# Gate biases of a recurrence: from three GpSimd additions to a one-hot matmul that opens the PSUM sum, and a wider clearance in the planner

## The chip, the cores and the metric

The kernel runs on one core of a Trainium2 chip. A core has five engines that run their own instruction queues in order and wait for each other through semaphores: TensorE (PE, matmuls into PSUM), VectorE (DVE), ScalarE (ACT), GpSimd (POOL) and SyncE (SP, which issues the DMAs here). The metric is the device time in microseconds of one execution of the whole program.

## The reference

Input `x` is 8 images of 56 x 56 pixels with 256 channels, all in float32. The program has two layers. Layer 0 normalizes in groups, routes each of the 49 regions (8 x 8 pixels) of an image to its 4 best regions, and does attention in which each query keeps only its 32 best of 256 keys; a 3 x 3 depthwise convolution of the values is added, and an output projection. Layer 1 sees the pixels of an image as a sequence of 3136 tokens: attention in a window of seven neighbours, then a recurrence over the tokens, each with a layer norm in front and a residual.

```python
def _L1_ffn_ref(x, U_i, V_i, b_i, U_f, V_f, b_f, U_c, V_c, b_c, U_o, V_o, b_o):
    xt = jnp.swapaxes(x, 0, 1)
    xi = xt @ U_i + b_i
    ...
    xg = xt @ U_c + b_c
    xo = xt @ U_o + b_o
    ...
    def step(carry, xs):
        h, c = carry
        xi_t, xf_t, xg_t, xo_t = xs
        i_t = jax.nn.sigmoid(xi_t + h @ V_i)
        f_t = jax.nn.sigmoid(xf_t + h @ V_f)
        g_t = jnp.tanh(xg_t + h @ V_c)
        o_t = jax.nn.sigmoid(xo_t + h @ V_o)
        c_new = h * c + i_t * g_t
        h_new = o_t * jnp.tanh(c_new)
        return ((h_new, c_new), h_new)
```

The gate `f_t` is computed and never used, so three gates are left. What the change touches are the input terms `xt @ U + b` of these three gates: 768 columns for each token.

## The kernel before

**Stages.** The work is cut into 56 units: seven rows of regions for each of eight images. A unit runs seven regions of the routed attention (scores on PE, eight rounds of MAX8 and MATCH_REPLACE8 on VectorE to find the 32 best, exponentials on ScalarE, a subtraction `pe - left` on GpSimd, lines 1004 and 1005, transposes and products on PE). A stream of "rows" steps follows a unit: output projection and residual (`project`; the bias `bo` is added to `x1` on GpSimd, line 1093), windowed attention (`window_attention`; the bias `bv1` is added on GpSimd, line 1192), layer norm, and at its end `gates(i)` for each block of 112 tokens (lines 1230 to 1252). `gates` transposes the normalized block (tile `xlT`), multiplies it with the gates' weights `wu` into two PSUM banks (512 and 256 columns, two matmuls each, since the 256 channels are two halves of the partitions), copies both on ScalarE to the tile `gs`, adds the bias `bu` in three GpSimd operations of 256 columns, and stores the block to DRAM (`xgd<-gs`). There are 224 such blocks, and 8 short ones of three tokens at the ends of the images. The banks come from `bank()`: two buffers for all of `rows`, `norm` (the first units' normalization, routing and keys) and the recurrence's output transposes.

**The recurrence** (lines 1338 to 1446) has 3136 steps in strict order, for all eight images at once. A step is a chain: `r_sum` (24 matmuls of the state with `r_v` into PSUM, on top of the input terms that were loaded back as `r_gin` and placed there), a tanh on ScalarE (`r_th`), a transpose on VectorE, a scan on VectorE (`r_c`, line 1394), a tanh on ScalarE (`r_tc`), and on VectorE the product that is the new state (`r_hs`, line 1405; called "the product" below). GpSimd then multiplies the new state with half the cell for the next step's scan (`r_cell<-r_hs,r_half`, line 1412). It starts once the first row of all eight images has its gates; from there on the steps run between the instructions of the attention, and the last ones run alone.

**The order is written out.** The class `_Plan` records every operation with a cost from `_time` (line 104: `held` is how long the engine is taken, `late` when the result is there) and lays all of them out in time by list scheduling (`run`, line 378); the order that comes out is the order of each engine's queue. On the chip only that order and the semaphores hold, not the planned times. In `run`:

- operations of the chain go as soon as they can; any other operation may start on an engine only if it would end by the time the chain is expected to need that engine, plus `SLACK` (line 63, 60 for GpSimd). For GpSimd the time that counts is that of the next chain operation with two SBUF operands, which is VectorE's scan or product, less `CLEAR` (lines 414 to 429).
- an operation of VectorE or GpSimd with two operands in SBUF that the plan itself made ("pair", line 341) is not started while the other engine runs one (line 449). Constants such as `bu`, `bo` and `bv1` are not the plan's tiles, so the three kinds of bias addition are not "pair".
- a GpSimd "pair" operation held over `LONG` may only start in the first part of a step (line 451).
- where PE would stand idle for more than `FILL`, a dummy matmul into `spare` is put in (lines 483 to 493 and 660 to 663). It computes nothing that is used.

`_halve` (line 520) halves the columns of two of the gates in `wu` and `bu`, since a sigmoid is computed as a tanh of half its argument.

Of the kernel before, what the change touches and what calls it, by code (L numbers as in the profile page):

```python
# [10 lines left out]
F32 = mybir.dt.float32  # L11
U32 = mybir.dt.uint32
AF = mybir.ActivationFunctionType
ALU = mybir.AluOpType
# [5 lines left out]
P = 128  # L20
C = 256
# [11 lines left out]
QB = 112  # L33
# [9 lines left out]
GATES = 3  # L43
# [15 lines left out]
FAR = 10**12  # L59
FILL = 220  # L60
LONG = 400
CLEAR = 250
SLACK = {"PE": 60, "DVE": 120, "ACT": 60, "POOL": 60, "SP": 1000}


# [174 lines left out]
class _Plan:  # L240
# [137 lines left out]
    def run(self, tc, fill):  # L378
# [35 lines left out]
        def expected(engine):  # L414
# [3 lines left out]
            for k in range(at, min(at + 7, len(chain))):  # L418
# [8 lines left out]
                if op.engine == engine or engine == "POOL" and op.pair:  # L427
                    return t - (CLEAR if engine == "POOL" else 0)
            return FAR
# [90 lines left out]
def _halve(nc, t, views):  # L520


    for v in views:
        for g in (1, 2):
            w = v.rearrange("p (j g u) -> p j g u", g=GATES, u=UJ)[:, :, g, :]
            nc.vector.tensor_scalar(w, w, 0.5, None, ALU.mult)
# [3 lines left out]
def _layers(ctx: ExitStack, tc, a, out):  # L530
# [9 lines left out]
    nc = tc.nc  # L540
    nb = x.shape[0]

    const = ctx.enter_context(tc.tile_pool(name="const", bufs=1))
# [14 lines left out]
    def bank():  # L558
        return ps_mm.tile([P, 512], F32, name="mm")
# [32 lines left out]
    def load(name, shape, src):  # L592
        t = const.tile(shape, F32, name=name)
        nc.sync.dma_start(t, src)
        return t
# [11 lines left out]

    bo = load("bo", [QB, C], a["bo"].to_broadcast((QB, C)))
    bv1 = load("bv1", [KB, C], a["bv1"].to_broadcast((KB, C)))
    bu = load("bu", [QB, GATES * C], a["br"].to_broadcast((QB, GATES * C)))  # L610
    _halve(nc, wu, [wu[:, k, :] for k in range(2)])
    _halve(nc, bu, [bu])

# [3 lines left out]
    for dy in range(3):  # L617
        rows = slice(dy * HD, (dy + 1) * HD)
        for n in range(24):
            k, dx, g = n // 12, n // 4 % 3, n % 4  # L620
# [28 lines left out]
    for t in sums:  # L649
        nc.tensor.matmul(  # L650
            t, gins[0].rearrange("p t g -> p (t g)")[:, :P], wu[:, 0, : t.shape[1]],
            start=True, stop=True, skip_group_check=True,
# [13 lines left out]
    raw, nc = nc, _Plan(tc)  # L666
# [396 lines left out]
    def layer_norm(i, src, by, nq=QB):  # L1063

        rs, off = by
        xl = two.tile([QB, C], F32, name="xln")
        nc.scalar.activation(
            xl[:nq], src, AF.Identity, bias=off[:nq, i : i + 1], scale=rs[:nq, i : i + 1]
        )
        pt = bank()  # L1070
        for k in range(2):
            nc.tensor.transpose(
                pt[:, k * QB : k * QB + nq], xl[:nq, k * P : (k + 1) * P], ident[:nq, :nq]
            )
        return pt[:, : 2 * QB].rearrange("p (k t) -> p k t", t=QB)[:, :, :nq]
# [58 lines left out]
    def window_attention(b, unit, im, row):  # L1134
# [95 lines left out]
        def gates(i):  # L1230
            q = sizes[i]
            xl = two.tile([P, 2, QB], F32, name="xlT")[:, :, :q]
            nc.scalar.copy(
                xl, layer_norm(i, row["t2"][:q, i, :], row["rs2"], q)
            )
            gs = two.tile([QB, GATES * C], F32, name="gs")[:q]
            for f, g in ((0, 2 * C), (2 * C, 3 * C)):
                pg = bank()
                for k in range(2):
                    nc.tensor.matmul(  # L1240
                        pg[:q, : g - f], xl[:, k, :], wu[:, k, f:g],
                        start=(k == 0), stop=(k == 1),
                    )
                nc.scalar.copy(gs[:, f:g], pg[:q, : g - f])
            for f in range(0, GATES * C, C):
                nc.gpsimd.tensor_tensor(
                    gs[:, f : f + C], gs[:, f : f + C], bu[:q, f : f + C], ALU.add
                )
            nc.sync.dma_start(
                xg[t0 // QB + i][:, :, b].rearrange("j g t u -> t (j g) u"),  # L1250
                gs.rearrange("t (j u) -> t j u", u=UJ),
            )
# [5 lines left out]
            + [lambda i=i: block(i) for i in blocks]  # L1258
            + [begin_gates]
            + [lambda i=i: gates(i) for i in blocks],  # L1260
        )

# [16 lines left out]
    for n in range(-(-SHIFTED // QB)):  # L1279
        q = min(QB, SHIFTED - n * QB)  # L1280
# [223 lines left out]
def _body(tc, a, out):  # L1504
    _layers(tc, a, out)
# [64 lines left out]
```

## Time and profile before

| what | value |
|---|---|
| time, median of 3 runs | 9194.27 us (9193.11 to 9199.71) |
| profiled execution, its own time | 9180.4 us |
| its span, first to last instruction | 9178.5 us |
| busy share of the span: PE, PE weight loads, DVE, ACT, POOL | 96%, 66%, 82%, 65%, 35% |
| granted clock of TensorE | 0.993 |
| bias additions `gs<-gs,bu` on POOL, full blocks | 672, mean 729 ns, busy 482.1 us |
| the same for the 8 short blocks | 24, mean 720 ns, busy 17.2 us |
| gates' matmuls, 512 columns, full blocks | 896 instructions, mean 636 ns, busy 491.9 us |
| gates' matmuls, 256 columns, full blocks | 896 instructions, mean 389 ns, busy 268.7 us |
| filler on PE (`spare<-ident`, line 661) | 14904 instructions, mean 276 ns, busy 2072.2 us |
| scan on DVE (`r_c<-r_cell`) | 3136, mean 290 ns, busy 910.8 us |

The trace is of one execution. "Busy" is the union of a group's instructions in time, so two overlapping instructions count once. A float32 matmul of the program shows as two instructions in the trace, and matmuls are pipelined, so their durations overlap. Every operation that the plan recorded has line 308, because the helper there issues them all; they are told apart by the names of their tiles (`out<-in`). The reason that is given for idle time is inferred from semaphores.

### The profile page before, as it was taken

How to read it: one execution, taken by the hardware profiler on the slowest of the kernel's cores; microseconds unless marked ns; L12 is line 12 of the kernel's file. 1: busy time of each engine (PE TensorE's matmuls, PEld its weight loads, DVE VectorE, ACT ScalarE, POOL GpSimd, SP SyncE). 2: the span in 40 equal slices, each digit the busy share in tenths (PEclk: the TensorE clock that was granted, in tenths of full speed). 3: DMA queues.
4: the chain of work that ended last, by engine and by line, in shares of the span. 5: the costliest groups of instructions: out<-in, count | busy, mean ns of one | idle time of the engine just before them, and what ended most of it. 6: DMA issues, size and time to landing. Idle time of an engine off the chain costs nothing.

```text
span 9178.5 us, 500794 instructions
## 1 busy us (share of the span) xinstructions
PE 8792.1 (96%) x203918; PEld 6037.0 (66%) x203918; DVE 7559.4 (82%) x32392; ACT 5939.4 (65%) x23551; POOL 3221.5 (35%) x7747
## 2 busy tenths in 40 slices
PE   7999999999999999999999999999999999999999
PEld 4555556666666666666666666666666666688888
DVE  5776799999999899999899999899999999734443
ACT  4665667776666677676676676677766766534444
POOL 1232344444343343343344443434434444311111
PEclk9999999999999999999999999999999999999999
DMA  6545433333332333333333333233333232210000
GB/s 198 155 129 163 111 106 82 93 92 80 93 91 78 91 84 90 89 85 91 88 82 92 91 82 90 78 93 88 83 92 89 80 90 78 60 28 23 23 24 21
DMA packets 1071271, 798.40 MB, mean 87 GB/s; under 512 B 402366, under 2 KB 1001524, under 8 KB 1068964
## 3 DMA queue, kind: packets, MB, share of 16 engines
q1 hardware_dynamic: 1068964, 766.36, 30.8%
q8 instruction: 1604, 26.28, 1.2%
q14 instruction: 703, 5.76, 0.2%
HBM read 527.08 MB, written 238.88 MB: 83 GB/s over the span
## 4 chain that ended last, share of the span: by engine, by line
PE 52%; DVE 25%; ACT 6%; issue 2%; DMA 1%; SPq 0%; POOL 0%; ACTq 0%; DVEq 0%; POOLq 0%
PE r_sum L308 19%; PE mm L308 15%; PE spare L661 12%; DVE left L308 8%; DVE top L308 6%; DVE r_c L308 3%; PE pt_av L308 3%; PE sc L308 3%; DVE r_cell L308 2%; DVE r_hs L308 2%; ACT pe L308 1%; ACT r_th L308 1%; ACT xln L308 1%; DVE st L308 1%; ACT r_sum L308 1%
## 5 line engine op out<-in xcount | busy, mean ns | idle before, releaser
L308 PE MATMUL r_sum<-r_v,r_hs 128*16 128x64 f32 (+2 forms) x150528 | 2758.0, 220 | 160.4 <-DVE r_hs L308 107.1
L308 PEld LDWEIGHTS r_sum<-r_v,r_hs 128*8 128x8 f32 (+2 forms) x150528 | 2224.2, 96 | 907.8 <-DVE r_hs L308 802.6
L308 POOL TENSOR_TENSOR r_cell<-r_hs,r_half 128x16 f32<-128x16 f32 x3136 | 706.7, 225 | 4012.7 <-DVE r_hs L308 3192.8
L661 PE MATMUL spare<-ident 128*32 128x128 f32 x14904 | 2072.2, 276 | 6.2 <-issue 4.5
L308 DVE MATCH_REPLACE8 left<-top,left 128x256 f32<-128x256 f32 x4704 | 1903.3, 408 | 0.0
L308 DVE MAX8 top<-left 128x8 f32<-128x256 f32 x4704 | 1848.2, 413 | 1.8 <-POOL r_cell L308 0.3
L308 ACT ACTIVATE r_th<-r_sum 128x64 f32<-128x64 f32 x3587 | 802.3, 224 | 1559.4 <-PE r_sum L308 1507.1
L661 PEld LDWEIGHTS spare<-ident 128*32 128x32 f32 x14904 | 1474.8, 110 | 309.6 <-issue 263.4
L308 DVE STREAM_TRANSPOSE r_cell<-r_th 128x64 f32<-128x64 f32 x3136 | 812.8, 259 | 882.5 <-ACT r_th L308 842.2
L308 POOL TENSOR_TENSOR pe<-pe,left 128x256 f32<-128x256 f32 x1568 | 1136.2, 729 | 821.5 <-ACT left L308 397.9
L308 ACT ACTIVATE r_tc<-r_c 128x16 f32<-128x16 f32 x3136 | 696.9, 222 | 717.4 <-DVE r_c L308 696.0
L308 DVE TENSOR_TENSOR_SCAN r_c<-r_cell 128x48 f32<-128x48 f32 x3136 | 910.8, 290 | 86.9
L308 ACT ACTIVATE pe<-sc,nmax 128x256 f32<-128x256 f32 x1568 | 710.9, 470 | 185.5 <-DVE left L308 105.3
L308 ACT ACTIVATE left<-left,nmax 128x256 f32<-128x256 f32 x1568 | 773.8, 502 | 13.8 <-DVE left L308 7.8
L308 PE MATMUL pt_av<-ident,pe 128*128 128x128 f32 x3136 | 691.2, 289 | 49.4 <-ACT pts L308 19.4
L308 PE MATMUL mm<-wu,xlT 128*112 128x256 f32 (+3 forms) x1856 | 732.6, 512 | 2.6 <-ACT xlT L308 1.7
L308 DVE MAX8 top<-sc 128x8 f32<-128x256 f32 x1568 | 620.4, 416 | 80.8 <-PE sc L308 80.4
L308 ACT ACTIVATE r_half<-r_c 128x16 f32<-128x16 f32 x3136 | 655.3, 209 | 0.0
L308 DVE SCALAR_TENSOR_TENSOR r_hs<-r_cell,r_tc 128x16 f32<-128x16 f32 x2685 | 545.4, 203 | 124.5 <-ACT r_tc L308 103.4
L308 DVE MATCH_REPLACE8 left<-top,sc 128x256 f32<-128x256 f32 x1568 | 641.2, 412 | 0.7 <-issue 0.6
L308 ACT COPY pts<-pt_av 128x256 f32<-128x256 f32 x1568 | 574.8, 367 | 97.6 <-PE pt_av L308 89.5
L308 PEld LDWEIGHTS pt_av<-ident,pe 128*128 128x128 f32 x3136 | 375.3, 143 | 349.2 <-issue 190.0
(131 smaller groups left out, 12151.6 us busy)
## 6 DMA issues: line engine op xcount, KB each, us to landing
kg<-kd SPq DMA_DIRECT2D x1568, 64.0 KB
vg<-vd SPq DMA_DIRECT2D x1568, 64.0 KB
vshift<-lines SPq DMA_DIRECT2D x336, 232.0 KB
xgd<-gs SPq DMA_DIRECT2D x224, 336.0 KB
r_gin<-xgd SPq DMA_DIRECT2D x1568, 48.0 KB
xchunk<-xt SPq DMA_DIRECT2D x112, 448.0 KB
lines<-v SPq DMA_DIRECT2D x112, 290.0 KB
xn<-xh SPq DMA_DIRECT2D x56, 560.0 KB
```

What stands on the lines that cost most here:

```text
L308: made[:] = [method(*[v.real() if isinstance(v, _View) else v for v in args], **{k: v.real() if isinstance(v, _View) else v for k, v in kw ...
L661: raw.tensor.matmul(spare[:32, :P], ident[:, :32], ident, start=True, stop=True, skip_group_check=True)
```

## The change

The additions on GpSimd are removed. Instead a constant matrix `bu` of 128 partitions holds the bias in its first row and zeros in the others, and a constant column `pick` is one in its first row and zero in the others. A matmul of `pick`, spread over the block's tokens, with `bu` gives the bias for each token; it opens the accumulation of each of the two PSUM banks (`start=True`), and the two matmuls of the weights add to it. The load of `bu` becomes one row in place of a copy to 112 partitions. Separately, the planner's constant `CLEAR` goes from 250 to 450.

```diff
-CLEAR = 250
+CLEAR = 450
...
-    bu = load("bu", [QB, GATES * C], a["br"].to_broadcast((QB, GATES * C)))
+    bu = const.tile([P, GATES * C], F32, name="bu")
+    nc.vector.memset(bu, 0.0)
+    nc.sync.dma_start(bu[0:1, :], a["br"])
+    pick = const.tile([P, 1], F32, name="pick")
+    nc.vector.memset(pick, 0.0)
+    nc.vector.memset(pick[0:1, :], 1.0)
...
             for f, g in ((0, 2 * C), (2 * C, 3 * C)):
                 pg = bank()
+                nc.tensor.matmul(
+                    pg[:q, : g - f], pick.to_broadcast((P, q)), bu[:, f:g], start=True, stop=False
+                )
                 for k in range(2):
                     nc.tensor.matmul(
                         pg[:q, : g - f], xl[:, k, :], wu[:, k, f:g],
-                        start=(k == 0), stop=(k == 1),
+                        start=False, stop=(k == 1),
                     )
                 nc.scalar.copy(gs[:, f:g], pg[:q, : g - f])
-            for f in range(0, GATES * C, C):
-                nc.gpsimd.tensor_tensor(
-                    gs[:, f : f + C], gs[:, f : f + C], bu[:q, f : f + C], ALU.add
-                )
             nc.sync.dma_start(
                 xg[t0 // QB + i][:, :, b].rearrange("j g t u -> t (j g) u"),
                 gs.rearrange("t (j u) -> t j u", u=UJ),
```

## The prediction

> **What bounds the kernel now.** I read the busy slices first, then the busy time by stage, then the groups of the middle stage, then the timeline around single steps.
>
> The slices of the span (40 equal ones, tenths busy) show three stages: a head without recurrence, a long middle, and a tail in which VectorE is 40% busy.
>
> ```profile
> PE   7999999999999999999999999999999999999999
> DVE  5776799999999899999899999899999999734443
> POOL 1232344444343343343344443434434444311111
> ```
>
> By stage (start:end, length, then busy us and instructions of PE, PEld, DVE, ACT, POOL, then granted clock, DMA share and GB/s):
>
> ```profile
> 0.00:1340.00 1340.00, 1191.84 (x8321) 705.94 (x8322) 975.89 (x3858) 796.82 (x2278) 393.82 (x732) 0.96 0.52 144
> 1340.00:7970.00 6630.00, 6399.55 (x162175) 4289.48 (x162173) 6107.11 (x26291) 4606.32 (x18589) 2672.57 (x6395) 1.00 0.32 87
> 7970.00:8230.00 260.00, 258.52 (x6841) 216.26 (x6840) 95.44 (x409) 98.94 (x465) 45.10 (x146) 1.00 0.12 32
> 8230.00:9178.00 948.00, 942.22 (x26589) 825.36 (x26586) 381.00 (x1837) 437.29 (x2222) 109.99 (x474) 1.00 0.08 23
> ```
>
> The middle holds 72% of the span (6630 of 9178.5) and there VectorE works 6107 of 6630 us. The trace has 2571 steps between 1345 and 7960 us, so 2.573 us a step; the tail has 443 steps in 940 us, 2.122 each. So the middle is bound by VectorE together with the serial chain of a step. PE's 6400 us are no bound: 1102.9 of them are filler.
>
> ```profile
> L661 PE MATMUL spare<-ident 128*32 128x128 f32 x7456 | 1102.9, 277 | 4.7 <-issue 4.5
> L308 PE MATMUL mm<-wu,xlT 128*112 128x512 f32 (+2 forms) x1560 | 619.0, 511 | 0.2
> ```
>
> What GpSimd costs is not its own time but what it does to two VectorE operations of the chain. Groups of the middle (xcount | busy, mean ns | idle before):
>
> ```profile
> L308 POOL TENSOR_TENSOR pe<-pe,left 128x256 f32<-128x256 f32 x1314 | 952.7, 729 | 283.2 <-ACT left L308 250.9 <-ACT pe L308 1.0 <-issue 0.3
> L308 POOL TENSOR_TENSOR gs<-gs,bu 112x256 f32<-112x256 f32 x567 | 408.1, 729 | 57.0 <-ACT gs L308 43.1 <-issue 1.6
> L308 DVE TENSOR_TENSOR_SCAN r_c<-r_cell 128x48 f32<-128x48 f32 x2571 | 773.8, 301 | 75.4
> L308 DVE SCALAR_TENSOR_TENSOR r_hs<-r_cell,r_tc 128x16 f32<-128x16 f32 x2571 | 525.1, 204 | 94.5 <-ACT r_tc L308 74.2
> L308 DVE MAX8 top<-sc 128x8 f32<-128x256 f32 x1310 | 522.1, 416 | 1.9 <-PE sc L308 1.5
> ```
>
> The same stage's medians are 258 ns for the scan and 175 for the product (r_hs): (301-258)*2571 = 110 us and (204-175)*2571 = 75 us are stalls. The timeline shows two of them (start, length): the scan stretched from 0.26 to 0.73 us beside a bias addition, the product from 0.18 to 0.44 beside a `pe` subtraction; each ends as GpSimd ends.
>
> ```profile
> 4808.89 0.73 POOL L308 TENSOR_TENSOR gs<-gs,bu 112x256 f32<-112x256 f32 x1
> 4809.01 0.73 DVE L308 TENSOR_TENSOR_SCAN r_c<-r_cell 128x48 f32<-128x48 f32 x1
> 5004.25 0.73 POOL L308 TENSOR_TENSOR pe<-pe,left 128x256 f32<-128x256 f32 x1 [1.62 <-ACT left L308]
> 5004.57 0.44 DVE L308 SCALAR_TENSOR_TENSOR r_hs<-r_cell,r_tc 128x16 f32<-128x16 f32 x1
> ```
>
> I went through the trace and put every scan or product over its median by 40 ns to the GpSimd operation beside it. Scans: `pe` 193 for 65.1 us, `gs` 141 for 34.5, `x` 32 for 9.3, `v` 9 for 2.6, `sum` 17 for 2.1. Products: `pe` 213 for 63.4, `v` 26 for 11.3, `gs` 27 for 3.7, `sum` 18 for 2.0, `x` 5 for 0.8. Together 194.8 us, `gs` 38.2 of it. This is all that the change can win on VectorE. A stall holds VectorE and the chain at once, so a microsecond saved is one off the end if the middle keeps its steps, and 2.12/2.57 = 0.83 if it keeps its length; I count 1.
>
> **The change, part by part.** *The additions go* (224 blocks of three, and 8 short blocks): 38.2 us of stalls with them. The other end is 0: the 204 steps of the middle with just one `gs` beside them average 2.432 us, those with no long operation 2.524, so there is no sign that an addition by itself costs a step. I take **-38**, the direct count.
>
> *Less crowding.* 48 scans were hit by a `pe` (12.3 us) and 28 by an `x` (8.1) that had started back to back behind another GpSimd operation. Without the additions that queue is shorter. **-20**; ends 0 and -20.
>
> *CLEAR 250 to 450.* In the plan the scan stands 231+925+260+276 = 1692 ns behind the product's start. A 256-column operation is held 728, so it may start up to 1692-250+60-728 = 774 ns behind the product, and after the change up to 574. But on the chip nothing ties GpSimd to the product: it starts when its queue and its data allow. The `pe` row waits 250.9 us for ScalarE's `left`, and the operation at 5004.25 started before the product that the plan puts it behind. A rule of the plan that lateness overrides should do little. Ends: all the rest of the stalls goes, -(194.8-38.2-20.4) = -136; or the 352 long operations that started 0.6 to 0.8 us behind a product's end are pushed into the next one at 63.4/213 = 0.30 us each, +105. I take **0**, between them. The new limit binds `nmax` and the power of the scales too (held 184 and 1050; the latter may start until 252 ns behind the product, before 452). `nmax` feeds ScalarE's `pe`, which frees the scores' banks; VectorE idles 1.5 us in the whole middle for new scores (the MAX8 row), for seven more rounds of work lie in between. With that cover gone it would be 656*0.2 = 131 us. Cost 0.
>
> The Trainium skill (SBUF — State Buffer, "Who interferes with whom") says that a VectorE operation with two SBUF inputs and a GpSimd operation that reads SBUF exclude each other, and that the one that issues second blocks until the first ends. A random hit on 729 ns would then cost 0.36 us, 168 hits of `gs` 61 us and the sum below -55; the trace's own hits average 38.2/168 = 0.23, so I keep the count.
>
> *The new matmuls.* Each block gets one more of 512 and one of 256 columns beside two of each, so half of the `mm<-wu,xlT` row: 619.0/2 = 310 us of PE in the middle, under the 1102.9 of filler. The cover is not perfect, since a matmul before `r_sum` delays it. From the product's end to the first `r_sum` matmul the fastest twentieth of the steps takes 54 ns, the mean 121: (121-54)*2571 = 172 us, caused by 6399.6-1102.9-2278.1 (the `r_sum` row) = 3019 us of other PE work, 0.057 each. 310*0.057 = **+18**. Ends: 0, and 390 matmuls each delaying a step by 0.28 (the worst class, 49 steps behind a 56-column `mm<-xn,w`: 333 ns in place of 54), +109. The first matmul of a group needs no `xlT`, so it waits for a bank alone and may take one of the two early, holding it through the 0.34 us `xlT` copy; behind it on PE stand `r_sum` and the scores. Nobody else of the middle uses these banks but `r_hx`'s transposes, once in 16 steps, for an output nobody waits for. Weights are loaded beside matmuls. In the price above.
>
> *Head.* 31 blocks by 491.9/448+268.7/448 = 1.70 us is 53 us more PE, where PE had 177 us of filler and 148 idle, and VectorE 364 idle. Between 53*0.057 = 3 and 53; nearer the lower, since PE's real work is (1192-177)/1340 = 76%. **+8**.
>
> *Start and queues.* One 3 KB row behind a memset in place of a 112-row load on SP; first use at 351 us. `xgd<-gs` on SP waits for ScalarE's copy and no longer for three additions: earlier, and the recurrence reads it a row of images later. 0. After 8070 us no gates are left: 0.
>
> **Sum:** -38-20+0+18+8 = -32 us. The profiled execution took 9180.4 (span 9178.5), so 9148; the median of the runs is 9194.27, 13.9 above it, so **9162**.
>
> **Rivals.** (a) *All collisions go*: -195+26 = -169, 9025. For it: 46% of the long operations start over 0.8 us behind a product, which a tighter rule is aimed at. Against: their data set their start. (b) *PE takes the place of GpSimd*: the new matmuls stand in front of `r_sum` at the worst class's price, +109 in the middle and +53 in the head, less 58: +104, 9298. It decides from (58-8)/390 = 0.13 us for each new matmul on. For it: PE without filler is 80% busy in the middle. Against: mean delay per step is 67 ns with four times as much work. (c) *The freed slots fill*: `pe` moves to where `gs` stood and meets the scan as often, so no stall goes: 0+26, 9220. For it: long operations number 2602 in 2571 steps, so slots are sought after; against: their own number falls by a fifth. (d) *Gains and costs cancel*, within 18 us.
>
> **How the numbers follow.** My forecast's case (-18 to -100) 0.42; (a) 0.10; (d) 0.16; (b) and (c) together 0.32. Two tenths of a per cent, 18 us, is about what this kernel's measurement tells from nothing. Faster 0.52, same 0.16, slower 0.32. The range 9070 to 9250 leaves 0.07 below, for most of (a), and 0.13 above, for (b); the forecast alone spans 9094 to 9176.
>
> **What would show it.** The scan's mean in the middle falls from 301 toward 285 ns, the product's stays near 204 (its stalls are `pe`'s lateness). Filler falls by about 300 us. Mean product-to-`r_sum` stays within 10 ns of 121. First `r_sum` of the recurrence at 1338 us moves under 15. Wrong if the scan and the product both drop to their medians, or if the step grows while filler is still there, or if the head grows by more than 40.

## The result, and the profile after

The changed kernel takes 9249.2 us (median of 5, 9239.2 to 9254.0), the kernel before 9194.3 on the same chip: a ratio of 1.0054, interval 1.0043 to 1.0065. It is slower, by 55 us; a gain of 32 had been forecast. The profiled execution has a span of 9252.1 us against 9178.5, 73.6 more: the one before lies 14 us under its median, the one after 5 us over its own.

The busy slices of the changed kernel, 40 equal ones:

```profile
PE   7999999999999999999999999999999999999999
DVE  5777799998888899898999998899899988844443
POOL 1222233333333333333333333333333323311111
```

VectorE's full stretch now lasts longer, and its fall to 4 comes later: the last MAX8 or MATCH_REPLACE8 of the attention ends at 8174 us in place of 7942. By stage (start:end, length, then busy time and instructions of the engines, granted clock, DMA share and rate):

```profile
0.00:1340.00 1340.00, 1212.06 (x8752) 710.77 (x8756) 988.44 (x3917) 812.47 (x2331) 334.03 (x653) 0.95 0.52 145
1340.00:7970.00 6630.00, 6428.14 (x160619) 4266.26 (x160609) 5961.75 (x25723) 4499.34 (x18242) 2205.24 (x5706) 1.00 0.32 85
7970.00:8230.00 260.00, 252.56 (x6377) 168.32 (x6366) 196.66 (x845) 159.67 (x665) 74.54 (x200) 1.00 0.24 63
8230.00:9178.00 948.00, 937.84 (x25331) 811.57 (x25332) 371.62 (x1774) 432.61 (x2153) 109.89 (x456) 1.00 0.10 25
```

VectorE is busy for less of the middle window than before (6107 us there): it gets less of the attention done in it. The two groups that the prediction was about, in the same window (busy, mean ns, idle before):

```profile
L308 DVE TENSOR_TENSOR_SCAN r_c<-r_cell 128x48 f32<-128x48 f32 x2568 | 734.5, 286 | 75.0
L308 DVE SCALAR_TENSOR_TENSOR r_hs<-r_cell,r_tc 128x16 f32<-128x16 f32 x2568 | 533.1, 208 | 117.7 <-ACT r_tc L308 100.8
```

The scan's mean has come down from 301 ns as forecast: the stalls beside the additions are gone. Counted as in the prediction, over the first 2500 steps, all stalls of scan and product fall from 189 to 161 us; the 36 us beside additions are gone, and those beside other GpSimd operations have grown by 8. The new matmuls on PE, all of them (count, then shortest, median and longest in ns, first and last in us, the commonest shapes), and then the filler in the middle window:

```profile
L308 PE MATMUL mm<-bu,pick x928: 378/591/1062, 348.1 to 8294.2; 128*112 128x256 f32 x92, 128*112 128x512 f32 x86, 128*3 128x512 f32 x8
```

```profile
L666 PE MATMUL spare<-ident 128*32 128x128 f32 x6576 | 962.6, 278 | 8.6 <-issue 8.5
```

A new matmul takes 0.59 us at the median, and the filler still has 963 us of the middle: by PE's room alone there was place for them.

I split the time of both profiles along the chain, step by step (first product; then, for the first 2500 steps, each wait and each operation; then the rest):

| us, total | before | after | difference |
|---|---|---|---|
| first product at | 1340.6 | 1316.3 | -24.3 |
| steps over 8 us, beyond 2.57 each | 0 | 24.4 | +24.4 |
| product's end to the first `r_sum` matmul | 303.6 | 383.7 | +80.1 |
| `r_sum` until the tanh starts | 2476.1 | 2452.2 | -23.9 |
| wait for the transpose | 224.8 | 208.3 | -16.5 |
| scan | 753.1 | 716.3 | -36.8 |
| product | 510.9 | 518.8 | +7.9 |
| wait for the second tanh | 188.3 | 176.2 | -12.1 |
| from step 2500 to the last product | 1398.0 | 1470.4 | +72.4 |

So the loss is not in the ordinary steps. Three steps wait long: 20.1 us at step 444, 9.4 at 1788 and 54.0 at 2684 (at 8234 us). Without what these take beyond 2.57 us, the first 2500 steps last 6435 us before and 6436 after: the 80 us more before `r_sum` are made up by the rows below it. The three waits are 76 us; another 21 come from the other steps after 2500, beside which the attention now runs on; the earlier start gives 24 back.

Step 2684 is followed by the first that needs tokens of the last row of regions. In the kernel before, the last gate copies of the seven rows were done at steps 1, 430, 865, 1301, 1733, 2168 and 2619, while the recurrence needs the rows' first tokens from steps 0, 445, 893, 1341, 1789, 2237 and 2685 on: up to the sixth row, every row gave it some 13 steps more of a lead. (The last row has one short block more for each image; its first blocks, which come into use first, were all done at 2608.) In the changed kernel the copies are done at 4, 448, 899, 1346, 1792, 2238 and 2691, and the last row's first blocks at 2685. The recurrence has caught up with its own input. The queue of SyncE shows it (start, length): the stores `xgd<-gs` stop, then the first block of the eighth image is stored, and right behind it the input terms `r_gin` of the next steps are loaded.

```profile
8204.22 23.23 SPq L308 DMA_DIRECT2D xgd<-gs  x4
8275.57 0.32 SPq L308 DMA_DIRECT2D xgd<-gs  x1
8278.86 3.14 SPq L308 DMA_DIRECT2D r_gin<-xgd  x8
```

Then ScalarE places the terms in PSUM, and `r_sum` starts again:

```profile
8284.85 0.48 ACT L308 COPY r_sum<-r_gin 128x128 f32<-128x128 f32 x2
8285.81 0.69 PEld L308 LDWEIGHTS r_sum<-r_v,r_hs 128*8 128x8 f32 x48 [0.77 <-ACT r_sum L308]
```

At 444 and 1788, too, the loads of the next terms begin only after the wait has begun (2467.2 and 5939.9 us; the waits begin at 2456.9 and 5937.5). These are the waits that ended last around step 2684:

```profile
POOL r_cell L308 <- DVE r_hs L308: 33.2, 7, 20.6
DVE r_cell L308 <- ACT r_th L308: 25.5, 7, 19.1
POOL v L308 <- ACT v L308: 24.3, 5, 11.5
```

Columns: engine and what waits, what it waits for, then total, times and longest in us. The chain's own pair, the copy on GpSimd behind the product and the scan behind the tanh, stands there seven times in these 70 us, where steps of 2.57 us would give 27, and the longest of them last 20.6 and 19.1 us: the engines of the recurrence stand idle. The waits name only the last releaser; that the gates are late is read from the gate copies, stores and loads above.

### The profile page after: what moved, and what is told of

It is laid out like the page before. It is cut to its first block, busy times and chain, and to the rows that moved or that the text cites. A ratio compares the mean times of both kernels' runs of the same rounds, so it can differ in the third digit from the quotient of the medians.

```text
span 9252.1 us, 498048 instructions
## 1 busy us (share of the span) xinstructions
PE 8899.4 (96%) x202968; PEld 6017.4 (65%) x202968; DVE 7546.9 (82%) x32395; ACT 5935.8 (64%) x23551; POOL 2732.1 (30%) x7051
## 4 chain that ended last, share of the span: by engine, by line
PE 59%; DVE 18%; ACT 6%; issue 2%; DMA 1%; POOL 0%; SPq 0%; ACTq 0%; DVEq 0%; POOLq 0%
PE r_sum L308 21%; PE mm L308 20%; PE spare L666 11%; DVE left L308 6%; DVE top L308 4%; PE pt_av L308 4%; PE sc L308 3%; DVE r_c L308 2%; DVE r_hs L308 2%; DVE r_cell L308 2%; ACT r_th L308 1%; ACT xln L308 1%; ACT pe L308 1%; ACT left L308 1%; ACT r_tc L308 0%
## 5 line engine op out<-in xcount | busy, mean ns | idle before, releaser
L308 PE MATMUL r_sum<-r_v,r_hs 128*8 128x64 f32 (+2 forms) x150528 | 2749.5, 220 | 156.4 <-DVE r_hs L308 92.7
L666 PE MATMUL spare<-ident 128*32 128x128 f32 x13026 | 1797.9, 276 | 10.2 <-issue 8.5
L666 PEld LDWEIGHTS spare<-ident 128*32 128x32 f32 x13026 | 1298.1, 110 | 244.3 <-issue 208.2
L308 DVE TENSOR_TENSOR_SCAN r_c<-r_cell 128x48 f32<-128x48 f32 x3136 | 872.6, 278 | 86.3
L308 PE MATMUL mm<-wu,xlT 128*112 128x256 f32 (+2 forms) x1856 | 744.6, 513 | 0.0
```

The costliest lines, as they stand in the source:

```text
L308: made[:] = [method(*[v.real() if isinstance(v, _View) else v for v in args], **{k: v.real() if isinstance(v, _View) else v for k, v in kw ...
L666: raw.tensor.matmul(spare[:32, :P], ident[:, :32], ident, start=True, stop=True, skip_group_check=True)
```

## Why the rows are late: reading the serial path

The "rows" stream has two banks and works through projection, windowed attention, gates, and then the next unit's values and convolution, one after the other. Mean over units 12 to 46 of four kernels, in us:

| stretch | before | after | matmuls, CLEAR 250 | no bias, CLEAR 250 |
|---|---|---|---|---|
| last addition to `sum` until the unit's first projection matmul | 34.3 | 58.8 | 41.1 | 49.0 |
| first projection matmul to first gate copy | 71.3 | 71.7 | 69.6 | 70.1 |
| first gate copy to last | 25.3 | 30.7 | 32.9 | 24.7 |
| last gate copy to the convolution of the next but one unit | 37.3 | 36.3 | 34.3 | 36.6 |
| convolution to the next unit's projection | 5.9 | 5.2 | 5.5 | 5.5 |

The last four follow each other without a gap and add up to the unit's time, 140.0 us before (sum of the rounded rows: 139.8). The first row says that the attention is done 34 us before its projection begins, so the attention is not what the rows wait for; it is the other way round, for the first addition to `sum` follows the convolution's copy by 0.1 to 0.9 us on average in these kernels. The rows' work is a serial path, and PE's filler hides nothing on it. The recurrence takes 448 steps of 2.57 us for a row of eight units, 143.9 us a unit, so this path had 3.9 us to spare. The new matmuls add 5.4 to 7.6 us to the gates' phase; the other stretches give part of it back. The whole unit takes 142.3 us with the matmuls alone, 143.4 with CLEAR alone (not in the table), and 143.9 with both: each part by itself leaves a little of the 3.9 us, both leave nothing. That this is why the two lose only together is argued from these means; a mean alone does not tell the loss, for one kernel below (matmuls, CLEAR 260) has 143.9 too and is not slow.

CLEAR lengthens the same path at another place. From the last mean and variance to the normalization that uses them (two GpSimd operations and one of VectorE lie between) it takes 2.83 us before, 3.64 after; 3.51 with CLEAR 450 alone, 2.87 with the matmuls alone. The power itself has the same length, only later; first the changed kernel's row in the middle, then that of the kernel before:

```profile
L308 POOL TENSOR_TENSOR rs<-rs,mhalf 112x4 f32<-112x4 f32 x85 | 88.1, 1037 | 5.0
```

```profile
L308 POOL TENSOR_TENSOR rs<-rs,mhalf 112x4 f32<-112x4 f32 x87 | 90.2, 1037 | 7.1
```

Both have a mean of 1037 ns: it is the start that CLEAR moves, not the length.

## The experiments

Ratios are to the kernel before, run beside each kernel; in brackets the 95% interval. That kernel took 9202.5 us beside the first four kernels below (the two parts apart) and 9191 to 9195 beside the others, so kernels of different groups are compared by ratio. "The wait" is that at step 2684 in the profile, which is one execution and not always a typical one.

**The two parts apart.** CLEAR alone, the matmuls alone, and no bias at all at both values (these two leave the gates' bias out).

```diff
-CLEAR = 250
+CLEAR = 450
```

> The kernel before with CLEAR 450 alone; the additions stay on GpSimd. Theory A (the new matmuls on PE take the loss, CLEAR does nothing): same as before, 9194 within 15 us, rows of gates done at steps 430, 865, 1301 as before. Theory B (the narrower GpSimd window takes the loss): as slow as the changed kernel, 9249, the attention ends near step 2660 and the recurrence waits for a row's gates at steps 444 and 2684. Theory C (each part slows the attention, and time is only lost where the recurrence then runs out of tokens): between, near 9220, with a wait at step 2684 shorter than the changed kernel's 54 us.

Measured: 9205.6, ratio 1.0003 [0.9994, 1.0012]; rows complete at 439, 887 and so on, the wait 17.9 us. Theory A has the time, but the rows are late and a wait is there, as C had it; ordinary steps that are 21 us shorter make up for part of it.

> The changed kernel with CLEAR back at 250: only the bias matmul is new. Theory A: 9249, as the changed kernel. Theory B: faster than before by the stalls beside the additions, about 9160 to 9180. Theory C: near 9200; the attention is slower than before, the recurrence waits at step 2684 for less than 54 us.

Measured: 9161.4, ratio 0.9949 [0.9935, 0.9963]: faster than before. Waits of 25.5 at step 444 and 19.5 at 2684, in a profiled execution of 9188.4 us, the slowest of the five; the other four took 9154 to 9163.

> Leaves the gates' bias out altogether (neither addition nor matmul), CLEAR 250: what the additions cost, without the price of their replacement. All theories: faster than before; by my count of stalls beside the additions 38 us and by less crowding 20 more, so 9136 to 9160. If the additions cost nothing of the end time: 9194.

Measured: 9180.5, ratio 0.9971 [0.9958, 0.9983]; no wait. This is above the 9136 to 9160 of the forecast: a gain of some 27 us where 58 had been counted.

> Leaves the gates' bias out altogether, CLEAR 450. Theory A: as with CLEAR 250. Theory B: slower than with CLEAR 250 by about 55 us. Theory C: without additions GpSimd has room, so slower than with CLEAR 250 by under 15 us, and no wait at step 2684.

Measured: 9164.7, ratio 0.9955 [0.9941, 0.9968]; no wait.

Where the time goes in these profiles, in us ("waits" is what steps over 8 us take beyond 2.57):

| | before | after | CLEAR alone | matmuls alone | no bias, 250 | no bias, 450 |
|---|---|---|---|---|---|---|
| first product at | 1340.6 | 1316.3 | 1353.6 | 1330.8 | 1335.1 | 1339.5 |
| first 2500 steps without waits | 6434.8 | 6435.8 | 6413.6 | 6393.7 | 6437.0 | 6429.1 |
| waits | 0 | 75.8 | 15.4 | 39.9 | 0 | 0 |
| steps from 2500 on without waits | 1398.0 | 1419.0 | 1419.1 | 1417.1 | 1380.3 | 1385.4 |

What follows: neither part is slow alone. The matmuls alone win 0.5%, CLEAR alone does nothing, CLEAR without any addition or matmul does no harm either, and the two together lose 0.54%. With the matmuls in, CLEAR costs 1% (0.9949 to 1.0054); at CLEAR 450 the matmuls cost 1% against no bias at all (0.9955 to 1.0054), and at 250 they cost nothing (0.9971 to 0.9949). Theories A and B fall. C had the direction, but its 9200 for the matmuls alone was 40 too high. Of the 66 us between the profiles of the changed kernel and of the matmuls alone, 36 are waits and 42 ordinary steps, less 15 at the start; why the steps are shorter at CLEAR 250 is open.

**More and less on PE.** The bias matmul cut to 8 columns and overwritten by the weights' product (this leaves the bias out), and issued twice.

```diff
-pg[:q, : g - f], pick.to_broadcast((P, q)), bu[:, f:g], start=True, stop=False
+pg[:q, :8], pick.to_broadcast((P, q)), bu[:, f : f + 8], start=True, stop=True
...
-                        start=False, stop=(k == 1),
+                        start=(k == 0), stop=(k == 1),
```

> The changed kernel, CLEAR 450, with the bias matmul cut to 8 columns and overwritten by the weights' matmul: the gates' bias is left out; the number, order and waits of the matmuls stay. Theory R (the matmuls' length lies on the serial path of the rows' work, which at 140.0 us a unit before was 3.9 us under the 143.9 that the recurrence leaves it): the gates' phase of a unit falls from 30.7 back to about 25 us, no wait at step 2684, 9160 to 9190. Theory S (a matmul that holds a bank early or blocks PE is what costs): as the changed kernel, 9249, with the wait.

Measured: 9232.7, ratio 1.0046 [1.0032, 1.0060]. As theory R wants, the gates' phase is 25.3 us, the rows are early (431, 862, ... 2579) and there is no wait; but the time is 43 us above R's range. The loss is in the steps: product to `r_sum` 393.0 us in the first 2500 steps, against 343.5 with no bias at all.

```profile
L308 PE MATMUL mm<-bu,pick x928: 169/243/354, 342.7 to 8016.3; 128*112 128x8 f32 x178, 128*3 128x8 f32 x8
```

The row gives a likely cause: the planner prices such a matmul at 5*8/3+50 = 63 ns, while its two instructions hold the next matmul back for about 130 ns (medians: 31 ns between their starts, 98 more to the next start; their lengths of 0.24 us overlap), so the planner squeezes it in front of `r_sum`. In 120 of the first 2500 steps the last matmul ahead of `r_sum` is one of the bias or one of the gates' weights behind it, and the gap is 36 us in all; with no bias it was 15 steps and 1 us. That is 35 of the 50 us more. Twice more, with other values of CLEAR:

> The short bias matmul (8 columns, overwritten; the gates' bias left out) with CLEAR 250. If the many short matmuls themselves cost (the bank taken early, PE's order): 9220 to 9245, as with 450. If 9233 was CLEAR's or the order's doing: as without any bias, 9155 to 9190. No wait at 2684 in either case.

Measured: 9275.0, ratio 1.0084 [1.0066, 1.0103]; rows early, no wait. This is above both forecasts, and the same count gives only 13 us here, so the gap before `r_sum` does not explain the slowest of the three.

> The same with CLEAR 440. If 9233 was a poor order and no mechanism: 9160 to 9210; if the short matmuls cost: 9220 to 9245. No wait at 2684.

Measured: 9229.3, ratio 1.0038 [1.0024, 1.0052]. So it was no poor draw of one order: the kernels with these short matmuls lose 0.4 to 0.8%, 35 to 77 us, to the kernel before without the rows being late. That their price in the plan is the cause is argued, for two of the three, and not shown; a kernel with the true price was not run.

> The matmul version with CLEAR 250 (9161), each bias matmul issued twice. Theory R: 6.4 us more in each of 48 units, nothing of it in slack, so some 300 us more, 9430 to 9520, with waits of about 50 us where each row of gates is late (steps near 444, 892, 1340, 1788, 2236, 2684). Theory of the prediction (PE has room, a new matmul costs the chain 0.057 of its length): +26, about 9190.

Measured: 9550.0, ratio 1.0393 [1.0377, 1.0409]. Waits of 42 to 61 us at steps 444, 892, 1340, 1788 and 2236, and 94 at 2684, as R forecast; the total is 30 above its range. The prediction's price for PE does not come near this. VectorE's slices show the starved middle:

```profile
DVE  5776788988898888989888888898988887854443
```

Only 6 of the slices are nines.

The bias of one group only by matmul:

```diff
+    ba = load("ba", [QB, GATES * C], a["br"].to_broadcast((QB, GATES * C)))
...
-                nc.tensor.matmul(
-                    pg[:q, : g - f], pick.to_broadcast((P, q)), bu[:, f:g], start=True, stop=False
-                )
+                if f == 512:
+                    nc.tensor.matmul(
+                        pg[:q, : g - f], pick.to_broadcast((P, q)), bu[:, f:g], start=True, stop=False
+                    )
...
+            for f in range(0, 2 * C, C):
+                nc.gpsimd.tensor_tensor(
+                    gs[:, f : f + C], gs[:, f : f + C], ba[:q, f : f + C], ALU.add
+                )
```

> CLEAR 250; the bias of the last 256 columns by matmul, that of the first 512 by two GpSimd additions as before. Theory R: 2.4 us more in a unit, within the 3.9 of slack: no wait at 444 or 2684, the attention ends between the two kernels, time between the kernel before and the full matmul version, 9150 to 9190. Theory of the prediction: a third of the gain, about 9180.

Measured: 9231.6, ratio 1.0044 [1.0030, 1.0058]. No wait and a gates' phase of 26.8 us, as R wants, yet slow: its first 2500 steps average 2.592 us, against 2.574 before. The scan's total is 751.1, so the additions left keep the stalls, and product to `r_sum` is 355.2. A miss for R's time; why its steps are slow stays open.

**Which GpSimd operations carry CLEAR's part.**

```diff
+PAIRED = 250
...
-                    if not op.chain and now + op.held > until:
+                    late = PAIRED - CLEAR if e == "POOL" and op.pair else 0
+                    if not op.chain and now + op.held > until - late:
```

> The changed kernel with CLEAR 450 for GpSimd operations that are no pair (nmax, the scales' two operations, the additions of bo and bv1, copies) and 250 for the pairs (pe, sum, r_cell). If the single ones carry CLEAR's loss (the scales stand on the rows' path: from mv to xln 2.87 us at 250, 3.64 at 450): 9225 to 9255, with the long wait at step 2684. If the pairs do: 9161 to 9180.

Measured: 9236.3, ratio 1.0048 [1.0035, 1.0062]; the wait 44.1 us, the scales 3.59 us.

> The changed kernel with CLEAR 450 for the pairs alone (pe, sum, r_cell) and 250 for GpSimd's other operations. The run with the reverse took 9236 and its scales 3.59 us from mv to xln. If the single operations carry CLEAR's loss: 9160 to 9180 here. If both carry some of it, or if the loss is the luck of a new order: 9200 to 9240, with the scales at 2.8 us all the same.

Measured: 9155.2, ratio 0.9967 [0.9953, 0.9981]; the wait 11.8 us, the scales 2.69 us. With the matmuls, a CLEAR of 450 costs where it binds the single operations, those that the planner does not hold to disturb VectorE's chain, and not where it binds the pairs: 0.8% lie between the two, from one order of each, about twice what a new order alone was worth (below). Its VectorE slices:

```profile
DVE  5777799888889989999999999989998988954443
```

They hold 20 nines against 17 of the changed kernel above, and the fall comes at the same slice of a span that is shorter.

> The changed kernel, CLEAR 450, but 250 for the two GpSimd operations of the layer norms' scales. If the scales' delay on the rows' path carries CLEAR's loss: mv to xln back at 2.8 us, the wait at step 2684 shorter than 30 us, 9155 to 9200. If nmax or the others do: 9225 to 9255.

Measured: 9215.0, ratio 1.0023 [1.0014, 1.0033]; scales 2.84 us, the wait 32.6.

> The changed kernel, CLEAR 450, but 250 for nmax alone. If nmax carries CLEAR's loss: 9155 to 9200, with the scales still at 3.6 us. If the scales do: 9225 to 9255.

Measured: 9224.4, ratio 1.0033 [1.0022, 1.0045]; scales 3.65 us, the wait 17.0, two others of 13 and 16. Neither is the whole: both times lie between the two forecasts, and the 0.2 to 0.3% taken back are less than a new order alone can be worth (next paragraph). With the scales spared, the path from mean to normalization is as short as before and a wait of 32.6 us is still there. Which of the single operations carry the loss stays open; the others were not tried.

**How much is the draw.** The planner's order changes everywhere with any constant, so neighbours of the values were run.

> The kernel before with CLEAR 260: nothing of the mechanism changes, only the order that the planner finds. It measures how far a new order alone moves the time. If little: 9191 within 10. If the order by itself is worth tens of microseconds, as the two kernels without any wait but 9232 suggest: anywhere in 9160 to 9230.

Measured: 9193.3, ratio 1.0002 [0.9992, 1.0012], as little as the first forecast had it.

> The matmul version with CLEAR 260 beside the one with 250 (9161). Theory R: the rows' work is late again, waits at steps 444 and 2684, the end after step 2500 over 1425 us as with all full matmuls (without them 1380 to 1398). If 9161 was the mechanism: 9150 to 9175. If it was a good draw: 9180 to 9220.

Measured: 9178.0, ratio 0.9988 [0.9978, 0.9998]; rows at 447, 900, 1344. Waits of 18.4 at step 444 and 11.2 at 1340, but none at 2684 and an end of 1405 us, not over 1425 as R wanted. The time lies between the two forecasts.

> The matmul version with CLEAR 440 beside the changed kernel (450, 9249). If the loss is the mechanism: 9235 to 9265, waits at 444 and 2684. If it was a bad draw: 9180 to 9230, the waits still there, but shorter.

Measured: 9227.8, ratio 1.0044 [1.0028, 1.0061]; the wait 32.6 us. The time is in the range forecast for a bad draw, but 0.44% is lost at 440 too, and by ratio that cannot be told from the changed kernel's 0.54%. A new order alone is worth nothing in the kernel before (1.0002) and 0.4% with the matmuls (0.9949 at 250, 0.9988 at 260). The matmuls with a CLEAR near 250, or 450 for the pairs alone, are faster than both kernels in all three runs (0.9949, 0.9988, 0.9967), the second only just.

## Why the prediction was wrong, point by point

- *The step that failed: the lateness of the gates, put at 0.* The prediction let the recurrence read the gates "a row of images later", and put the queues at 0 and CLEAR's delay of `nmax` and of the scales at 0 for the cover of VectorE's seven rounds. The lead was 15 steps for the first row and grew by some 13 a row, or 3.9 us a unit, and both parts of the change draw on it. With both, the recurrence waits 76 us for its gates, more than the 73.6 us between the two profiles. The terms were priced apart and added; they do not add: CLEAR costs nothing without the matmuls (1.0003) and 1% with them (0.9949 to 1.0054; from 260 to 440, 0.9988 to 1.0044).
- *The additions go, -38, less crowding, -20*: the stalls went as counted, 36 us beside additions, and the scan lost 36.8 us. The crowding's 20 did not come: stalls beside other operations grew by 8. That a stall saved is a microsecond off the end failed: the first 2500 steps without waits are no shorter, 6434.8 before and 6435.8 after, nor 6437.0 with no bias at all.
- *The new matmuls, +18*: as a price on the chain it was about right. A bias matmul runs between the product and `r_sum` in 104 of the first 2500 steps, and these gaps are 24 us in all. Most of the gap's growth by 80 us is something else: some 40 comes with no bias at all (347.3 and 343.5, against 303.6), since the transposes of `pe` stand last before `r_sum` more often once the additions are gone (721 and 739 steps against 577, and their gaps grow from 90 us to 135 and 140; 731 steps and 142 us after). What was wrong is that filler covers them: they stand on the rows' serial path and lengthen the gates' phase by 5.4 to 7.6 us a unit.
- *CLEAR, 0*: right for the kernel before (ratio 1.0003) and for the pairs. Wrong together with the matmuls, through the single operations. Among them are the scales, which wait on the rows' path and not on VectorE's, so the seven rounds were the wrong cover for them; how much of the loss is theirs stays open.
- *Head, +8*: it was 24 us shorter. With matmuls at full length, issued once, the first product comes between 1308 and 1331, without any bias at 1335 to 1340, so here the order that the planner found did it; which part of the order stays open.
- *The signs*: the scan's 285 and the product's 204 came (286 and 208). The filler fell by 140 us and not 300, the mean from product to `r_sum` rose by 32 ns and not under 10, and the recurrence started 24 us earlier. Of the signs of being wrong, only the step grew, by 0.01 us in its mean over the first 2500, and that is the waits.
- *Luck*: the matmuls with CLEAR 250 took 9161, the 9162 of the forecast, but by other ways: in their profile the steps are 41 us shorter, the waits 40 longer and the end 19 longer. At 260 it was 9178.
- *Rivals*: (b) named PE as the new bound, with the new matmuls standing in front of `r_sum`, at 9298. The gap there grew, but a new matmul was the last before `r_sum` in only 24 steps, 2.6 us in all, so its mechanism is not what happened. (c) kept the stalls, and they went. The late rows were in no rival.

## What to carry to other kernels

An engine's filler or idle time hides new work only if nothing serial waits for that work: before pricing an operation by its engine's room, follow its own stream and ask how much earlier than needed its result comes, here some 13 steps a row or 3.9 us a unit. Two edits that each cost nothing can lose together when both draw on such a reserve, so test them apart and together. And a safety margin in a scheduler is best bound only to the operations that it protects against: here the pairs, not everything on the engine.

## What was not expected of the hardware

A GpSimd addition that stretches a scan or product shows no stretch itself: the additions' durations lie between 711 and 767 ns in all 696 cases, while a scan beside one took up to 784. The recorded length of a matmul says little of what a short one costs: the two instructions of the 8-column bias matmul took 0.24 us each (median 243 ns), but the second starts 31 ns after the first and the weights' matmul 98 ns after that; at 512 columns, with 0.64 us each, these distances are 434 and 429 ns, and at 256 columns, with 0.38 us, 216 and 216.
